# Four stacked graph layers on one core: partial sums of the projections copied by ScalarE from PSUM bank to PSUM bank, and layer 0's bias put into PSUM ahead of its products

## The chip, the cores and the metric

The kernel runs on one core of one Trainium2 chip. A core has five engines with queues of their own: TensorE (PE, with its weight loads shown as PEld), VectorE (DVE), ScalarE (ACT), GpSimd (POOL) and SyncE (SP, which here only issues DMAs). Matmul results land in PSUM, eight banks of 128 partitions by 512 fp32 elements; everything else lies in SBUF. The metric is the device time of one execution in microseconds, lower is better.

## What is computed

128 graphs of 128 nodes with 512 features pass four layers; after each layer the result is added to its input and every row is normalised:

```python
x = _layernorm(x + _L0_gnn_ref(x, adj, L0_kernel, L0_bias))   # relu(An @ x @ W0 + b0)
x = _layernorm(x + _L1_gnn_ref(x, adj, L1_W_qk, L1_W_v))      # softmax over nodes of a score, times x @ Wv
x = _layernorm(x + _L2_gnn_ref(x, adj, L2_W))                 # relu([x, Ar @ x] @ W2)
x = _layernorm(x + _L3_gnn_ref(x, adj, L3_W, L3_b))           # An @ (x @ W3 + b3)
```

All of it is fp32. The large cost is the product of a 128-node block of features with a 512 by 512 weight, once per graph in layers 0, 1 and 3 and twice in layer 2.

## The kernel before

Work comes in 32 tiles of four graphs. For each tile the kernel aggregates (`aggregate`: features times the normalised adjacency, PSUM tile `p_agg`, evicted by ACT into `agg`), or turns the features (`turn_x` through DMAs and DVE transposes, `turn_on_tensor` on TensorE, tiles `xT`), and then projects. The aggregations and turnings of layer L deliver the left operand of the projection of layer L.

The projections save one matmul in eight. Four graphs are taken as a 2 by 2 arrangement (two graph rows r, two pairs q), features and weights are split in halves, and instead of eight block products seven are made, named `B11, T1, B21, B22, T2, T3, T4`. Three of the left operands are sums of blocks, made by `left_sums`: S1 (for T1), S2 (for T2), S4 (for B22), each a chain step after the one before. POOL makes them in the ordinary tiles, DVE in some of the first and last ones. The sums of the weights are made once, by `weight_sums`. What the savings cost is that several results share partial sums: B11 goes into all four result blocks.

`project` (lines 583 to 650) does this for layers 0, 2 and 3 (`o0`, `o2`, `o3`; PSUM tiles `p_o`, 128x512, both pairs in one bank). Each product is 8 matmul records of 128x256 per weight (16 in layer 2, which has two weights). Before the change, the shared partial sum is carried through SBUF: ACT copies B11's sum into `s`, DVE then adds PSUM sums and SBUF sums:

```python
product(g, B11, True);  sa, sb = first(g, block)      # ACT copy (l0: two POOL adds of the bias)
product(q, T1, True);   u5 = q + sb                   # VectorE
product(v, T2, True);   u2 = v + sb                   # VectorE
product(q, B22, False); u2 = q + u2                   # VectorE
product(v, T3, False);  u5 = v + u5                   # VectorE
product(p, T4, ...);    sa = p + sa                   # VectorE, deferred to the tail
```

B21 is accumulated onto B11 in `g`, right after B11 where `early` holds (layers 0 and 2, and the last tile of layer 3), and after T1 elsewhere. The product T4 and what follows it is deferred: it is put on the list `tails` and run by `finish_tails()` after the next stage's B11. `fin` adds a result block to `x` (with relu in layers 0 and 2), `norm_stats` and `norm_last` normalise.

`l1_out` (lines 789 to 833) is the same scheme for the attention layer, with 320 output columns (256 values and 64 for the score), one bank for each pair q. It runs each of the seven products for both pairs before the next product (2 matmuls, 4 records of 128x320, per pair and product).

The order on TensorE is the order of the Python program. On the other engines it is not: `Plan` records all operations, and its list scheduler (`schedule`, `run`) orders DVE, ACT, POOL and SP by due times that it computes from estimated durations. Hooks (`{T1: [...]}`) place pieces of other stages between the products of a projection. In the ordinary tiles, layer 0 of tile t, layers 2 and 3 of tile t-1 and layer 1 of tile t are interleaved; `begin()` (tiles 0 to 2) and the lines after the loop (tile 31, `last`) have orders of their own. There, `l2_both` makes the aggregations and the turned features on TensorE and `left_sums` runs on DVE.

PSUM: the pool `ps_b` has five banks (`pb`), `ps_t` three (`pt`). At the start, `WARM` transposes of the identity run on TensorE while the first data are loaded.

Of the kernel before, what the change touches and what calls it, by code (L numbers as in the profile page):

```python
# [15 lines left out]
P = 128  # L16
# [9 lines left out]
DEG_EPS = 1e-6  # L26
WARM = 30

# [318 lines left out]
def estimate(engine, method, args, kw):  # L347

    out = args[0]
    n = out.idx.size if isinstance(out, Ref) else 0  # L350
    if engine == "tensor":
        return (max(109, 0.85 * n) if method == "transpose" else 2 * max(104, 0.833 * n + (2.5 if n > P else 5))), 100, 0, False
    if method == "dma_start":
        size = max(int(np.prod(v.shape)) if isinstance(v, bass.AP) else v.idx.size * 32 * len(v.quads) for v in args)
        return 470, Plan.LAND + size / 60, size, False
    if engine == "scalar":
        return (380 if method == "activation" else 160) + 0.83 * n, 0, 0, False
    if engine == "gpsimd":
        return (400 + 150 * n if ALU.pow in args else 250 + 2 * n), 0, 0, True
    if method in ("bn_stats", "tensor_reduce"):  # L360
        n = args[1].idx.size
    both = [v for v in args[1:] if isinstance(v, Ref) and v.idx.size == n and v.tile.args[3]["tag"] not in ("pb", "pt")]
    return 160 + (1.12 if len(both) > 1 else 1.04) * n, 0, 0, len(both) > 1
# [3 lines left out]
def kernel(  # L367
# [71 lines left out]
    make_identity(tc.nc, ident.real())  # L439
    p = ps_t.tile([P, C, P], FP, tag="pt", name="p_warm")  # L440
    for _ in range(WARM):
        nc.tensor.transpose(p[:, 0], ident, ident)
    nhalf = const.tile([P, G], FP, tag="nhalf", name="nhalf")
# [3 lines left out]
    w0_sb = weight(w0, "w0_sb", nc.sync)  # L447
    b0_sb = broadcast_row(b0, "b0_sb", nc.sync)
    wqk_sb = tp.tile([P, C, 2 * ATT], FP, tag="row", name="wqk_sb", bufs=1)
    for b in range(Q):  # L450
# [131 lines left out]

    def project(name, t, parts, first, c11, fin, hooks=None, after=lambda: None, pairs=(0, 1), early=True):

        hooks = hooks or {}
        qs = slice(pairs[0], pairs[-1] + 1)

        def region():  # L590
            return ps_b.tile([P, 2, H], FP, tag="pb", name=f"p_{name}_{t}")[:, qs]

# [5 lines left out]

        def product(p, k, fresh):
            with nc.unit():  # L600
# [9 lines left out]
        def block(tag):  # L610
            return tp.tile([P, 2, H], FP, tag=tag, name=f"{tag}_{name}_{t}", bufs=2 if tag == "s" else 1)[:, qs]

        g, q, v = region(), None, None
        product(g, B11, True)
        sa, sb = first(g, block)
        finish_tails()
        if early:
            product(g, B21, False)
            c11(g, block)
        q = region()  # L620
        product(q, T1, True)
        u5 = block("u5")
        nc.vector.tensor_tensor(u5, q, sb, ALU.add)
        if not early:
            product(g, B21, False)
            c11(g, block)
        v = region()
        product(v, T2, True)
        u2 = block("u2")
        nc.vector.tensor_tensor(u2, v, sb, ALU.add)  # L630
        product(q, B22, False)
        nc.vector.tensor_tensor(u2, q, u2, ALU.add)
        fin(0, 1, u2)
        norm_stats(name, t, 0, pairs)
        product(v, T3, False)
        nc.vector.tensor_tensor(u5, v, u5, ALU.add)
        fin(1, 1, u5)

        def tail():
            p = v  # L640
            if (name, t, pairs[-1]) == ("o3", last, 1):
                nc.vector.tensor_tensor(sa, v, sa, ALU.add)
                p = region()
            product(p, T4, p is not v)
            nc.vector.tensor_tensor(sa, p, sa, ALU.add)
            fin(1, 0, sa)
            norm_stats(name, t, 1, pairs)
            after()
# [3 lines left out]
    def half(z, r, h, pairs=(0, 1)):  # L652

        return z.rearrange("p (q r) f -> p q r f", r=2)[:, pairs[0]:pairs[-1] + 1, r, h * H:(h + 1) * H]

    def copy_first(p, block):
        s = block("s")
        nc.scalar.copy(s, p)
        return s, s


# [66 lines left out]
    def l0_out(t, hooks=None, pairs=(0, 1)):  # L728
        fin = relu_add(t, pairs)

        def bias(h):
            return b0_sb[:, None, h * H:(h + 1) * H].to_broadcast([P, len(pairs), H])

        def first(p, block):
            sa, sb = copy_first(p, block)[0], block("sb")
            nc.gpsimd.tensor_tensor(sb, sa, bias(1), ALU.add)
            nc.gpsimd.tensor_tensor(sa, sa, bias(0), ALU.add)
            return sa, sb

        def c11(p, block):  # L740
            c = block("u2")
            nc.vector.tensor_tensor(c, p, bias(0), ALU.add)
            fin(0, 0, c)

        project("o0", t, [("agg0", w0_sb)], first, c11, fin, hooks, pairs=pairs)

# [42 lines left out]
    def l1_out(t, hooks):  # L789
# [11 lines left out]
        st["v", t] = out  # L801
        s = out[1, 0]

        def region():
            return [ps_b.tile([P, 2, H], FP, tag="pb", name=f"p_v_{t}_{q}").rearrange("p a b -> p (a b)")[:, 0:V]
                    for q in range(2)]

        def product(p, k, fresh, then):
            for q in range(2):
                with nc.unit():  # L810
                    for c in range(2):
                        nc.tensor.matmul(p[q], a[k][:, q, c, :], wv_sb[:, c, k, :], start=(fresh and c == 0),
                                         stop=(c == 1), skip_group_check=True)
                then(p[q], q)
            for f in hooks.get(k, ()):
                f()

        def add(to, other):
            return lambda p, q: nc.vector.tensor_tensor(to[:, q, 0:V], p, other[:, q, 0:V], ALU.add)

        for r in range(2):
            nc.scalar.copy(out[r, 1][:, :, V], st["d", t].rearrange("p (q r) -> p q r", r=2)[:, :, r])
        g = region()
        product(g, B11, True, lambda p, q: nc.scalar.copy(s[:, q, 0:V], p))
        finish_tails()
        q5 = region()
        product(q5, T1, True, add(out[1, 1], s))
        product(g, B21, False, lambda p, q: nc.scalar.copy(out[0, 0][:, q, 0:V], p))
        v = region()
        product(v, T2, True, add(out[0, 1], s))  # L830
        product(q5, B22, False, add(out[0, 1], out[0, 1]))
        product(v, T3, False, add(out[1, 1], out[1, 1]))
        product(v, T4, False, add(s, s))

# [41 lines left out]
    def l2_out(t, hooks=None, pairs=(0, 1)):  # L876
        fin = relu_add(t, pairs)
        project("o2", t, [("xT2", w2x_sb), ("agg2", w2a_sb)],
                copy_first, lambda p, b: fin(0, 0, p), fin, hooks, pairs=pairs)


    def l3_agg(t):
        left("agg3", t)
        for g in (0, 1, 3, 2):
            aggregate("agg3", t, g, st["anT", t], 2 if g == 2 else 1)
        left_sums("agg3", t)

# [12 lines left out]
    def l3_out(t, hooks=None, left="agg3", pairs=(0, 1)):  # L900
        def fin(r, h, blk):
            z = half(st["x", t], r, h, pairs)
            nc.vector.tensor_tensor(z, blk, z, ALU.add)

        project("o3", t, [(left, w3_sb)], copy_first, lambda p, b: fin(0, 0, p), fin, hooks,
                after=lambda: store(t), pairs=pairs, early=t == last)

# [8 lines left out]
    def begin():  # L916
# [14 lines left out]
        l1_turn(0, turn_on_tensor, (1,))  # L931
        l1_out(0, {T3: [lambda: l1_turn(1, turn_on_tensor)]})
        l1_out(1, {B11: [lambda: l1_scores(0)], T1: [lambda: l1_softmax(0)], B21: [lambda: l1_add(0)]})
        l2_both(0, 0)
        l2_out(0, {B11: [lambda: l2_both(0, 1), lambda: prep(2)], T1: [lambda: l1_scores(1)], T2: [lambda: l1_softmax(1)], T3: [lambda: l1_add(1)]})
        l0_agg(2)
        l2_turn(1)
        l0_out(2, {B21: [lambda: l2_agg(1, 0)], T1: [lambda: l2_agg(1, 1)]})
        l3_agg(0)
# [10 lines left out]
    for t in range(2, NT):  # L950
        u = t - 1
        if t > 2:
            l0_out(t, {T1: [lambda: l2_agg(u, 0)], T2: [lambda: l2_agg(u, 1)]})
        tails.append(lambda: l1_turn(t))
# [7 lines left out]
        l3_bias(u)  # L962
        l3_out(u, {B11: [lambda: l1_softmax(t)], B21: [lambda: l1_add(t)]})
        if t < last:
# [4 lines left out]
    for q in range(2):  # L969
        l2_out(last, {B11: [lambda: l2_both(last, 1)], B21: [held]} if q == 0 else {B22: [lambda: l3_agg_pair(last, 0, nc.gpsimd)]}, (q,))  # L970
    for q in range(2):
# [37 lines left out]
```

## Time and profile before

| | before |
|---|---|
| time, median of 3 runs | 2437.45 us (2437.34 to 2437.57) |
| profiled execution, first to last instruction | 2436.3 us |
| PE busy | 2426.0 us (100%), 12462 records |
| PEld busy | 2090.2 us (86%) |
| DVE busy | 1637.9 us (67%) |
| POOL busy | 1219.3 us (50%) |
| ACT busy | 1004.2 us (41%) |
| mean granted TensorE clock | 1.000 |

The profile tells of one execution. Its span runs from the first to the last instruction and is 1.15 us shorter than the median time, which also holds what lies around the instructions. In the groups of the profile a line reads: engine, operation, output tile <- input tiles, shapes, count, busy time, mean duration of one in ns, idle time before it and who ended that idle time. All recorded operations carry the line of one helper (L323), so tiles tell them apart. Every fp32 matmul stands as two records; transposes stand as one.

### The profile page before, as it was taken

What the parts mean: (1) busy time and instruction counts of PE and PEld (TensorE: products, weight loads), DVE (VectorE), ACT (ScalarE), POOL (GpSimd) and SP (SyncE); (2) the same over time, 40 slices, a digit from 0 to 9 for tenths busy, and PEclk for the clock granted to TensorE, in tenths of its full rate; (3) what the DMA queues carried; (4) which work ended last, traced back from release to release, by engine and by line L of the source; (5) the groups of instructions that cost most, each with busy time, mean ns of one, the idle gap of its engine ahead of it and who ended that gap; (6) DMA issues with size and microseconds to landing.
All of it is one profiled execution on the core that took longest, in us unless ns stands there. A gap on an engine that the chain in (4) does not pass through costs nothing.

```text
span 2436.3 us, 35723 instructions
## 1 busy us (share of the span) xinstructions
PE 2426.0 (100%) x12462; PEld 2090.2 (86%) x12462; DVE 1637.9 (67%) x3398; ACT 1004.2 (41%) x2117; POOL 1219.3 (50%) x1580
## 2 busy tenths in 40 slices
PE   9999999999999999999999999999999999999998
PEld 8888888888888888888888888888888888888887
DVE  6766666677666677666776667666677666676656
ACT  4344333443434444344443444433443434444345
POOL 5364545545445554545455554545545455554543
PEclk9999999999999999999999999999999999999999
DMA  5234233442334433344333343333442334423220
GB/s 182 47 101 109 70 105 94 126 124 64 99 92 126 126 78 83 97 120 126 90 80 100 109 126 104 74 104 95 126 121 66 100 91 126 126 74 88 75 82 35
DMA packets 393267, 241.16 MB, mean 99 GB/s; under 512 B 140416, under 2 KB 358016, under 8 KB 393088
## 3 DMA queue, kind: packets, MB, share of 16 engines
q1 hardware_dynamic: 393088, 238.88, 36.4%
q8 instruction: 99, 1.62, 0.3%
q14 instruction: 80, 0.66, 0.1%
HBM read 126.62 MB, written 112.20 MB: 98 GB/s over the span
## 4 chain that ended last, share of the span: by engine, by line
PE 99%; ACT 1%; DVE 0%; POOL 0%; issue 0%; POOLq 0%; ACTq 0%; DVEq 0%
PE p_o L323 63%; PE p_v L323 20%; PE p_agg L323 14%; PE p_sc L323 1%; PE p_warm L323 0%; PE p_xT L323 0%; DVE x L323 0%; ACT x L323 0%; PE p_ws L323 0%; PE p_w L323 0%; ACT xT L323 0%; ACT xT1y L323 0%; POOL agg L323 0%; POOL last L323 0%; PE p_a L323 0%
## 5 line engine op out<-in xcount | busy, mean ns | idle before, releaser
L323 PE MATMUL p_o<-w_sb,agg 128*128 128x256 f32 x2048 | 471.0, 380 | 0.6 <-DVE u_o L323 0.6
L323 PEld LDWEIGHTS p_o<-w_sb,agg 128*128 128x128 f32 x2048 | 386.1, 190 | 52.0 <-POOL rstdv L323 1.0
L323 ACT COPY agg<-p_agg 128x512 f32<-128x512 f32 (+1 forms) x415 | 226.4, 554 | 371.9 <-PE p_agg L323 371.8
L323 PE MATMUL p_v<-wv_sb,xT 128*128 128x320 f32 x1024 | 291.6, 433 | 0.1
L323 DVE TENSOR_TENSOR v<-p_v,v 128x320 f32<-128x320 f32 x316 | 155.0, 491 | 174.7 <-PE p_v L323 174.4
L323 PE MATMUL p_o<-w2x_sb,xT 128*128 128x256 f32 x1024 | 263.1, 379 | 0.5 <-ACT xT L323 0.5
L323 PE MATMUL p_o<-w2a_sb,agg 128*128 128x256 f32 x1024 | 262.8, 379 | 0.0
L323 PEld LDWEIGHTS p_v<-wv_sb,xT 128*128 128x128 f32 x1024 | 192.0, 190 | 76.5 <-ACT xT L323 0.6
L323 PEld LDWEIGHTS p_agg<-anT,x 128*128 128x128 f32 x2048 | 238.7, 192 | 7.1 <-DVE anT L323 0.6
L323 PE MATMUL p_agg<-anT,x 128*128 128x128 f32 x2048 | 239.3, 275 | 0.3 <-DVE anT L323 0.3
L323 DVE TENSOR_TENSOR u_o<-p_o,u_o 128x512 f32<-128x512 f32 (+1 forms) x196 | 131.4, 672 | 149.1 <-PE p_o L323 149.1
L323 PEld LDWEIGHTS p_o<-w2x_sb,xT 128*128 128x128 f32 x1024 | 194.0, 190 | 30.7 <-ACT xT L323 1.0
L323 PEld LDWEIGHTS p_o<-w2a_sb,agg 128*128 128x128 f32 x1024 | 194.6, 190 | 26.4
L323 PE MATMUL p_v<-wv_sb,xT1s 128*128 128x320 f32 x768 | 217.2, 432 | 0.0
L323 PE MATMUL p_o<-w2x_sb,xT2s 128*128 128x256 f32 x768 | 197.1, 379 | 0.0
L323 PE MATMUL p_o<-w2a_sb,agg2s 128*128 128x256 f32 x768 | 197.1, 379 | 0.0
L323 ACT ACTIVATE x<-x,nmro,rstdo 128x512 f32<-128x512 f32 x256 | 195.2, 808 | 3.4
L323 PEld LDWEIGHTS p_v<-wv_sb,xT1s 128*128 128x128 f32 x768 | 145.7, 190 | 57.3
L323 PE MATMUL p_o<-w_sb,agg0s 128*128 128x256 f32 x768 | 180.8, 379 | 0.0
L323 DVE TENSOR_TENSOR u_o<-p_o,s_o 128x512 f32<-128x512 f32 (+1 forms) x132 | 88.5, 671 | 131.4 <-PE p_o L323 131.3
L323 PE MATMUL p_o<-w_sb,agg3s 128*128 128x256 f32 x744 | 170.8, 379 | 0.0
L323 DVE BATCH_NORM_STATS2 bno<-x 128x6 f32<-128x512 f32 x258 | 168.1, 683 | 3.3
(147 smaller groups left out, 4021.7 us busy)
## 6 DMA issues: line engine op xcount, KB each, us to landing
x<-in_x_dram SPq DMA_DIRECT2D x31, 1024.0 KB, 5.7
out_dram<-x SPq DMA_DIRECT2D x31, 1024.0 KB, 5.0
xT2s<-x SPq DMA_DIRECT2D x120, 256.0 KB, 2.5
xT2y<-xT2s SPq DMA_DIRECT2D x240, 128.0 KB, 3.3
xT1s<-x SPq DMA_DIRECT2D x120, 256.0 KB, 2.6
xT1y<-xT1s SPq DMA_DIRECT2D x240, 128.0 KB, 3.1
sa<-ana SPq DMA_DIRECT2D x120, 128.0 KB, 3.4
ya<-sa SPq DMA_DIRECT2D x120, 128.0 KB, 3.0
```

The lines of the kernel that those rows point to most:

```text
L323: op.ins = getattr(getattr(self.nc, op.engine), method)(*[v.real() if isinstance(v, Ref) else v for v in args], **{k: v.real() if isinstan ...
```

## The change

Partial sums are now carried inside PSUM. ACT copies a bank to another bank, and later products are accumulated onto the copy (matmuls without the start flag). In `project`, the product order becomes B11, (tails), T1, T2, B21, B22, T3, and T4 in the tail: `x` is a copy of B11's bank and takes T2, then `y`, a copy of `x`, takes B22, while `x` itself goes on to take T3 and T4; B21 goes onto B11's own bank. T1's result `f` is copied to SBUF by ACT and added by DVE once per result block of the last column. In layer 3 (`fold`) `f` is added to both blocks of `x` in one DVE operation instead, and the results are then added straight from PSUM. Layer 0's two bias halves (the second as a difference, made by one DVE subtraction at the start) are put into PSUM by two ACT copies ahead of B11 and T1; its two POOL additions per tile go away. The separate bank for the very last T4 goes away too.

`l1_out` takes each pair q as a generator of its own; the two are stepped in a fixed interleaving, fresh products use `ps_t`, copies use `ps_b`, and the last T4 becomes a tail, run by a new `finish_tails()` inside `l3_agg`. Hooks of the neighbouring stages are moved to other products. `WARM` goes from 30 to 28, and these transposes now write the banks of `ps_b`, in turn.

Over the program, ACT has 452 copies more (1195 for 743), DVE 551 tensor additions fewer (616 for 1167), POOL 64 fewer (1250 for 1314); TensorE has 6316 matmuls and transposes for 6318.

```diff
-WARM = 30
+WARM = 28
...
-    for _ in range(WARM):
-        nc.tensor.transpose(p[:, 0], ident, ident)
+    for i in range(WARM):
+        p = ps_b.tile([P, C, P], FP, tag="pb", name="p_warm") if i % C == 0 else p
+        nc.tensor.matmul(p[:, i % C], ident, ident, start=i % C == 0, stop=True, is_transpose=True, skip_group_check=True)
...
+    nc.vector.tensor_tensor(b0_sb[:, H:F], b0_sb[:, H:F], b0_sb[:, 0:H], ALU.subtract)
...
+        def copied(p):
+            to = region()
+            nc.scalar.copy(to, p)
+            return to
+
+        if seeds is None:
+            r = region()
+            product(r, B11, True)
+            x = copied(r)
+        else:
+            x, w = region(), region()
+            nc.scalar.copy(x, seeds[0])
+            nc.scalar.copy(w, seeds[1])
+            product(x, B11)
+            r = copied(x)
         finish_tails()
+        if seeds is None:
+            w = region()
+        product(w, T1, seeds is None)
+        f = block("f")
+        nc.scalar.copy(f, w)
+        if fold is not None:
+            fold(f)
+        product(x, T2)
+        y = copied(x)
+        product(r, B21)
+        fin(0, 0, r)
+
+        def last_column(p, r):
+            if fold is not None:
+                return fin(r, 1, p)
+            u = block("u")
+            nc.vector.tensor_tensor(u, p, f, ALU.add)
+            fin(r, 1, u)
+
+        product(y, B22)
+        last_column(y, 0)
         norm_stats(name, t, 0, pairs)
+        product(x, T3)
+        last_column(x, 1)
 
         def tail():
+            product(x, T4)
+            fin(1, 0, x)
             norm_stats(name, t, 1, pairs)
...
+        def one(q):                       # l1_out, one pair
+            p = fresh(B11, q)
+            x = copied(p, q)
+            yield
+            w = fresh(T1, q)
+            f = tp.tile([P, V], FP, tag="f", name=f"f_v_{t}_{q}", bufs=2)
+            nc.scalar.copy(f, w)
+            product(x, T2, q)
+            y = copied(x, q)
+            yield
+            product(p, B21, q)
+            end(0, 0, q, p)
+            yield
+            product(y, B22, q)
+            end(0, 1, q, y, f)
+            product(x, T3, q)
+            end(1, 1, q, x, f)
+            yield
+            product(x, T4, q)
+            end(1, 0, q, x)
+            yield
...
         for g in (0, 1, 3, 2):
             aggregate("agg3", t, g, st["anT", t], 2 if g == 2 else 1)
+            finish_tails()
...
-        l1_out(1, {B11: [lambda: l1_scores(0)], T1: [lambda: l1_softmax(0)], B21: [lambda: l1_add(0)]})
+        l1_out(1, {(T1, 0): [lambda: l1_scores(0)], (B21, 0): [lambda: l1_softmax(0)], (B22, 0): [lambda: l1_add(0)]})
...
-        l2_out(last, {B11: [lambda: l2_both(last, 1)], B21: [held]} if q == 0 else {B22: [lambda: l3_agg_pair(last, 0, nc.gpsimd)]}, (q,))
+        l2_out(last, {B11: [lambda: l2_both(last, 1)], T1: [held]} if q == 0 else {B22: [lambda: l3_agg_pair(last, 0, nc.gpsimd)]}, (q,))
```

## The prediction

> **What bounds the kernel now.** First the page: busy times and the chain that ended last.
>
> ```profile
> span 2436.3 us, 35723 instructions
> ...
> PE 2426.0 (100%) x12462; PEld 2090.2 (86%) x12462; DVE 1637.9 (67%) x3398; ACT 1004.2 (41%) x2117; POOL 1219.3 (50%) x1580
> ...
> PE 99%; ACT 1%; DVE 0%; POOL 0%; issue 0%; POOLq 0%; ACTq 0%; DVEq 0%
> ```
>
> TensorE is the chain. A busy PE may still hide gaps, so the second view is a window one period long in the middle (busy time and count of PE, PEld, DVE, ACT, POOL, then clock and DMA).
>
> ```profile
> 1200.00:1275.26 75.26, 75.26 (x388) 64.89 (x387) 50.66 (x106) 30.89 (x65) 38.23 (x50) 1.00 0.37 102
> ```
>
> The chain in order of time repeats every 75.26 us (p_v at 1227.39, then 1302.65), with PE busy throughout. That is its work: 224 records of p_o at 0.216 us apart (48.4), 56 of p_v at 0.269 (15.1), 96 of p_agg at 0.112 (10.7), scores and two small transposes 1.1. The third view, TensorE's waits, says what is left to gain:
>
> ```profile
> PE p_warm L323 <- POOL ident masks.py:199: 1.3, 1, 1.3
> PE p_xT L323 <- ACT xT1y L323: 0.7, 1, 0.7
> PE p_o L323 <- DVE u_o L323: 0.6, 1, 0.6
> PE p_o L323 <- ACT xT L323: 0.5, 2, 0.3
> PE p_agg L323 <- DVE anT L323: 0.3, 1, 0.3
> PE p_agg L323 <- ACT x L323: 0.2, 1, 0.2
> ```
>
> 3.6 us, all in the first tiles or the last; behind the last matmul there are 6.5 us more (2429.7 to 2436.3). The change keeps TensorE's work. It can win only there, and can lose wherever PE comes to wait.
>
> **Ordinary tiles: 0.** Per tile ACT gets 8 more copies of 128x512 and 6 of 128x320, DVE loses 12 additions of 128x512 and 6 of 128x320 and gets one of 1024 columns, POOL loses two bias additions. By the rows
>
> ```profile
> L323 ACT COPY s_o<-p_o 128x512 f32<-128x512 f32 (+1 forms) x98 | 56.5, 577 | 179.6 <-PE p_o L323 179.5
> L323 ACT COPY v<-p_v 128x320 f32<-128x320 f32 x128 | 54.5, 426 | 211.2 <-PE p_v L323 211.2
> L323 POOL TENSOR_TENSOR s_o<-s_o,b_sb 128x512 f32<-128x512 f32 x32 | 40.7, 1272 | 23.0 <-DVE x L323 23.0
> ```
>
> ACT goes from 30.9 to 30.9 + 8 x 0.58 + 6 x 0.43 = 38 of 75.26 us; DVE falls by 12 x 0.69 + 6 x 0.49 - 1.3 = 9.9, POOL by 2.5. None becomes the bound. No row shows a copy from PSUM to PSUM: the nearest are the 577 ns above and 611 ns from SBUF to SBUF (xT1y<-x); I take 0.58, bounds 0.43 (the short copy) and 0.81 (ACT's longest 128x512 operation).
>
> What counts is each hand-over: PE to ACT 0.25 us after the last matmul's slot (p_o's B11 ends at 1246.29, s_o starts at 1246.54), copy 0.58, back to PE 0.05 (anT ends at 8.87, p_agg starts at 8.92): 0.88. The copy of B11 must be done by T2, behind T1's 8 x 0.216 = 1.73, in layer 2 3.45; the copy y by B22, behind B21, the same. Slack 0.85 at the worst copy bound still 0.6, if ACT is free; the order of the changed program puts nothing long before these copies. In layer 1: 0.2 + 0.43 + 0.05 = 0.68 against 2.15 (two products of 1.08). The tightest wait is no copy: the second pair's T4 stands only 8 records of p_agg (0.89) behind T3, whose bank DVE must read first: 0.21 (T2's slot ends 1232.60, DVE starts 1232.81) + 0.49 + 0.05 = 0.75. Slack 0.14, DVE being idle there. Layer 2's T1 now comes without B21 (3.45 us) before it; its S1 on POOL ended 3.3 us early (xT2s 1274.88 + 1.27, T1 at 1279.49). DVE's lighter queue starts it earlier: about 1 us of slack stays.
>
> **Start: +0.2.** Two transposes fewer take 0.22 (two at the full rate, 0.11 as in p_a) to 0.43 (0.213, as most warm-ups ran) off the 12.60 at which B11 starts. But B11 now waits for a seed: b_sb, which landed at 3.97 + 8.3 = 12.25, is issued one place earlier (11.1, where the second w_sb landed), and its copy stands on ACT behind the third agg copy (11.90, now 11.7): 11.7 + 0.48 + 0.58 + 0.05 = 12.8. Bounds -0.2 and +0.5.
> [...]
>
> **Layer 1 of tile 0: +0.1.** T1 stands behind one pair's B11 (1.08), not two. S1 needs, after the last turn, 0.25 + 0.58 + 0.12 + 1.27 + 0.05 = 2.3, so PE waits 1.2, and 0.24 at T2 (S2 costs 1.32 against 1.08). In return the wait for xT1y (0.87 with its restart) and 0.4 of small ones go: ACT's chain there hung on POOL, which loses 1.27 of bias work.
>
> **Layer 1 of tile 1: +0.5, then +0.45.** Before, T1 at 64.34 stood 5.1 us after the last turn (59.19); now 2.15, at 61.3. xT1s ended at 62.17: 0.9 at most, 0.15 if POOL's weight sums before it move up. Tile 0's scores are hooked later: from p_w to layer 2's p_agg stood 11.0 us of PE work (66.55 to 77.54), now 9.8, and the chain (softmax, add, norm on ACT until 76.81) takes 10.3.
>
> **Layer 2 of tile 0: +0.6.** DVE's xT2s ends at 88.47; B21 covered it (86.86 to 90.32). Now only one T4 of layer 1 does: 86.86 + 1.08 = 87.94. Bounds 0.5 and 1.1.
>
> **Layer 3 of tile 0: +0.4.** S2 on POOL (131.16 to 132.79, T2 at 136.70) loses the cover of B21 (1.73) and of the tail moved ahead (1.73), and POOL also waits for DVE (0.72 in its row). Bounds 0 and 0.6.
>
> **Layer 2 of the last tile: +1.75.** The widest:
>
> ```profile
> 2389.55 1.03 PE L323 MATMUL p_o<-w2x_sb,xT 128*128 128x256 f32 x4
> ...
> 2390.83 0.69 DVE L323 TENSOR_TENSOR xT2s<-xT 128x512 f32<-128x512 f32 x1 [0.35 <-ACT xT L323]
> ...
> 2391.27 1.89 PE L323 MATMUL p_o<-w_sb,agg 128*128 128x256 f32 x8
> ...
> 2393.00 0.81 PE L323 MATMUL p_o<-w2x_sb,xT2s 128*128 128x256 f32 x3
> ```
>
> B21 (2389.55) and the held T4 (2391.27) cover S1, which ends at 2391.52. In the new order T1 comes first, and the held T4 behind it. PE would wait from 2389.55 to 2391.57; the s_o copy that stood before the last copies on ACT (0.26) comes after them now: 1.75, bounds 1.5 and 2.0.
>
> **End: +0.2.** The last T4 goes onto the bank that DVE is still reading: 0.2 + 0.42 + 0.05 = 0.7 of wait (before, a fresh bank). Behind it one DVE addition less: -0.45.
>
> **Dropped: -0.2.** The wait of 0.6 for u_o goes, but the next one, for ACT's x, is set by a chain that does not move.
>
> Sum: 0.2 + 0.1 + 0.5 + 0.45 + 0.6 + 0.4 + 1.75 + 0.2 - 0.2 = 4.0. On the profiled 2436.3 that is 2440.3; with the 1.15 us that the median lies above it, 2441.4. The lower bounds sum to +1.1, the upper to +6.5. The measurement tells 0.2% from no change, 4.9 us: 2432.6 to 2442.3.
>
> [...]
>
> **The rivals.** (1) Slower by a wait in every tile: T4 of layer 1 (slack 0.14) or S1 of layer 2 (about 1 us, behind a DMA whose landing varies). For it: the thin slack, and DVE's read being last. Against: PE had no such wait in 30 tiles at 0.33 of slack. It decides from 0.14 us of lateness on; 0.3 us late would be 30 x 0.3 = 9 on top, 2450. Chance 0.08. (2) Slower within the edges: the waits at first and last tiles come out at their upper bounds, 2443 to 2444; from +4.9 on it counts as slower. Chance 0.23. (3) Faster: the lighter DVE and POOL remove PE's early waits and the new ones stay hidden. All of PE's waits (3.6), the tail's 0.45, 0.4 of warm-up and the restarts (1.1) make -5.5 at most, 2432; the view of the last tile speaks against it. Chance 0.04. (4) The change does less than it says, because PE's order leaves the copies no use: nothing but the edges, which is the forecast.
>
> **How the numbers follow.** The forecast, within 0.2%, has 0.65; slower 0.08 + 0.23 = 0.31; faster 0.04. The range runs from the lower bounds (2438.5) to the upper (2444), and a little beyond toward rival 1: 2438.4 to 2444.6.
>
> **What would show it.** PE busy per 75.26 us unchanged and no wait of PE between 180 and 2300; ACT near 38, DVE near 41 us per period; a PE wait near 2391 for DVE's xT2s of 1.5 to 2 us, one of 0.7 before the last T4, some of 0.3 to 1.2 for POOL and DVE before 140. A PE wait repeated in each tile, or a copy beyond 1.4 us, would make it wrong.

## The result, and the profile after

The changed kernel takes 2443.21 us (median of 10 runs, 2442.83 to 2444.23) against 2437.47 us (10 runs, 2437.32 to 2438.33): ratio 1.0024, 95% interval 1.0014 to 1.0033. It is slower by 5.7 us, just past the 4.9 us that the prediction called measurable; the forecast was 2441.4 and the range 2438.4 to 2444.6. The profiled execution took 2442.89 us.

The page after: span, busy time, and the chain that ended last.

```profile
span 2441.1 us, 35406 instructions
...
PE 2426.6 (99%) x12460; PEld 2088.7 (86%) x12460; DVE 1365.1 (56%) x2847; ACT 1212.1 (50%) x2569; POOL 1156.4 (47%) x1516
...
PE 97%; POOL 1%; DVE 1%; ACT 1%; issue 0%; DMA 0%; POOLq 0%; ACTq 0%; DVEq 0%
```

TensorE's work is unchanged (2426.6 for 2426.0), ACT has 208 us more, DVE 273 us less, and the span is 4.8 us longer. The window of one period in the middle, columns as before:

```profile
1200.00:1275.26 75.26, 75.26 (x388) 64.89 (x387) 42.04 (x89) 37.47 (x79) 36.44 (x47) 1.00 0.40 102
```

PE is 100% busy, with the same 388 records in 75.26 us. 8.6 us less DVE and 6.6 us more ACT per tile are worth nothing. The 4.8 us stand in TensorE's waits:

```profile
PE p_o L323 <- DVE xT2s L323: 2.0, 2, 1.6
PE p_warm L323 <- POOL ident masks.py:199: 1.3, 1, 1.3
PE p_agg L323 <- ACT x L323: 1.0, 2, 0.7
PE p_v L323 <- POOL xT1s L323: 1.0, 1, 1.0
PE p_a L323 <- DVE ana L323: 0.7, 1, 0.7
PE p_o L323 <- POOL agg3s L323: 0.6, 1, 0.6
...
PE p_o L323 <- DVE x L323: 0.5, 1, 0.5
PE p_o L323 <- ACT p_o L323: 0.3, 1, 0.3
```

Each stands once or twice, so none belongs to an ordinary tile. Three of the eight name a sum of operands (xT2s, xT1s, agg3s), and one a bank that is still being read (x: the last T4). `p_agg` waits for x, normalised by ACT, once behind the later scores of tile 0 and once in the last tile. `p_warm` waits as before, and the 0.7 us ahead of `p_a` stand behind warm-ups that ended early in this execution; B11 began at 12.48 all the same, 12.60 before. Only `ACT p_o`, 0.3 us for the first seed, waits for a copy. The largest wait, on the timeline of the last tile:

```profile
2392.93 0.69 DVE L323 TENSOR_TENSOR xT2s<-xT 128x512 f32<-128x512 f32 x1 [0.35 <-ACT xT L323]
...
2393.66 0.69 DVE L323 TENSOR_TENSOR xT2s<-xT2s,xT 128x512 f32<-128x512 f32 x1
2393.68 0.30 PEld L323 LDWEIGHTS p_o<-w2x_sb,xT2s 128*128 128x128 f32 x2 [1.84 <-DVE xT2s L323]
```

T1 starts as S1 ends. DVE is no later than before relative to what it waits for (0.35 us of idle time in both); the products that had covered it, that is, had kept PE busy meanwhile, stand behind T1 now. The price of the new copies, from the groups by shape:

```profile
L323 ACT COPY p_o<-p_o 128x512 f32<-128x512 f32 x188 | 107.8, 573 | 249.3 <-PE p_o L323 249.3
L323 ACT COPY p_v<-p_v 128x320 f32<-128x320 f32 x128 | 52.5, 410 | 78.1 <-PE p_v L323 77.9
```

The copy from bank to bank takes 573 ns, where the prediction took 0.58 us, and the narrow one 410.

### The profile page after: what moved, and what is told of

It reads as the page before. It is cut to its first block, busy times and chain, and to the rows that moved or that the text cites. A ratio compares the mean times of both kernels' runs of the same rounds, so it can differ in the third digit from the quotient of the medians.

```text
span 2441.1 us, 35406 instructions
## 1 busy us (share of the span) xinstructions
PE 2426.6 (99%) x12460; PEld 2088.7 (86%) x12460; DVE 1365.1 (56%) x2847; ACT 1212.1 (50%) x2569; POOL 1156.4 (47%) x1516
## 3 DMA queue, kind: packets, MB, share of 16 engines
q1 hardware_dynamic: 393088, 238.88, 37.5%
## 4 chain that ended last, share of the span: by engine, by line
PE 97%; POOL 1%; DVE 1%; ACT 1%; issue 0%; DMA 0%; POOLq 0%; ACTq 0%; DVEq 0%
PE p_o L323 63%; PE p_v L323 19%; PE p_agg L323 14%; PE p_sc L323 1%; DVE x L323 0%; POOL xT1s L323 0%; POOL w_sb L323 0%; ACT xT L323 0%; ACT agg L323 0%; PE p_ws L323 0%; PE p_w L323 0%; ACT x L323 0%; DMA ana<-in_adj_dram 0%; POOL w2a_sb L323 0%; ACT xT2y L323 0%
## 5 line engine op out<-in xcount | busy, mean ns | idle before, releaser
L323 PE MATMUL p_o<-w_sb,agg 128*128 128x256 f32 x2048 | 476.8, 380 | 0.8 <-DVE x L323 0.5
L323 DVE SCALAR_TENSOR_TENSOR x<-p_o,x 128x512 f32<-128x512 f32 (+1 forms) x130 | 88.7, 683 | 405.2 <-PE p_o L323 402.4
L323 PE MATMUL p_v<-wv_sb,xT 128*128 128x320 f32 x1024 | 307.2, 433 | 0.0
L323 PEld LDWEIGHTS p_agg<-anT,x 128*128 128x128 f32 x2048 | 243.6, 192 | 11.8 <-DVE anT L323 0.4
L323 PE MATMUL p_agg<-anT,x 128*128 128x128 f32 x2048 | 244.2, 275 | 0.2 <-DVE anT L323 0.2
L323 ACT COPY p_o<-p_o 128x512 f32<-128x512 f32 (+1 forms) x196 | 110.7, 565 | 255.8 <-PE p_o L323 255.8
L323 PE MATMUL p_v<-wv_sb,xT1s 128*128 128x320 f32 x768 | 228.3, 433 | 1.1 <-POOL xT1s L323 1.0
L323 POOL TENSOR_TENSOR xT1s<-xT 128x512 f32<-128x512 f32 x32 | 40.7, 1273 | 277.4 <-DVE xT L323 250.4
```

The costliest lines, as they stand in the source:

```text
L323: op.ins = getattr(getattr(self.nc, op.engine), method)(*[v.real() if isinstance(v, Ref) else v for v in args], **{k: v.real() if isinstan ...
```

## The experiments

Each edits the changed kernel, except before_t1_first. Theory: the ordinary tiles cost nothing, and the loss is cover taken from operand sums, and one bank, at the first and last tiles (the edges). Rival: something per copy or per tile that the waits do not show.

**held_first.** One piece of PE work changes place.

```
-        l2_out(last, {B11: [lambda: l2_both(last, 1)], T1: [held]} if q == 0 else {B22: [lambda: l3_agg_pair(last, 0, nc.gpsimd)]}, (q,))
+        l2_out(last, {B11: [lambda: l2_both(last, 1), held]} if q == 0 else {B22: [lambda: l3_agg_pair(last, 0, nc.gpsimd)]}, (q,))
```

> The changed kernel, with one piece of TensorE work moved: in the last tile the held T4 of layer 3 (8 records of p_o, 1.73 us of PE) stands ahead of layer 2's T1 instead of behind it. Theory (the loss is cover taken from the operand sums): the wait of 1.76 us for DVE's xT2s at 2393.68 goes, with the 0.10 us of restart behind it; xT2s is then ready within 0.1 us of PE. Span 2441.1 - 1.8 = 2439.3, median near 2441.4. Rival (DVE's queue is late as a whole, so that the wait only moves to T2, which needs the next xT2s and agg2s): 0 to -0.5, median 2442.7 to 2443.2.

Measured: 2441.83 (2441.14 to 2442.48), ratio 1.0018 (1.0009 to 1.0026); span 2439.3, 1.8 less than the changed kernel's. T1 started at 2393.63 against S1's end, with a wait below 0.1. The span is the theory's number (the median is 0.4 above its 2441.4), and no wait reappeared at T2. One line of order was worth a quarter to a third of the loss (1.4 by the medians, 1.8 by the spans).

**t4_fresh.** The last T4 gets a bank of its own.

```
         def tail():
-            product(x, T4)
-            fin(1, 0, x)
+            p = x
+            if (name, t, pairs[-1]) == ("o3", last, 1):
+                fin(1, 0, x)
+                p = region()
+            product(p, T4, p is not x)
+            fin(1, 0, p)
```

> The changed kernel, but the very last T4 goes onto a PSUM bank of its own, and DVE adds both banks, one after the other, to the output rows. Theory: the wait before the last T4 (0.68 us, and 0.10 of restart) goes; DVE's additional 0.42 us runs beside T4's 0.86. Median 0.7 to 0.8 lower, 2442.4; TensorE's end 2434.9 - 0.78 = 2434.1, the tail stays at 6.2. Rival (the additional DVE operation lengthens the tail by as much): 0, median 2443.2.

Measured: 2443.25 (2442.84 to 2443.74), ratio 1.0024 (1.0014 to 1.0033): no gain. PE's wait is gone as expected (its last records follow one another at 0.216), yet the tail behind PE's end grew from 6.2 to 6.7 us. B11 of tile 0 also happened to start 0.76 later in this execution (below), so its times compare after taking 0.76 off. ACT's last sum of squares and POOL's instructions near the end, first of the changed kernel, then of this one:

```profile
2435.24 0.19 ACT L323 ACTIVATION_READ_ACCUMULATOR square<-x,last 128x1 f32 x1
...
2435.51 0.19 POOL L323 TENSOR_SCALAR last<-last 128x1 f32<-128x1 f32 x1 [1.56 <-ACT square L323]
...
2436.22 0.22 POOL L323 TENSOR_SCALAR rstdo<-mvo 128x1 f32<-128x1 f32 x1 [0.52 <-DVE mvo L323]
2436.40 0.57 POOL L323 TENSOR_TENSOR last<-last,nhalf 128x1 f32<-128x1 f32 x1
```

```profile
2436.03 0.19 ACT L323 ACTIVATION_READ_ACCUMULATOR square<-x,last 128x1 f32 x1
...
2436.35 0.22 POOL L323 TENSOR_SCALAR rstdo<-mvo 128x1 f32<-128x1 f32 x1 [1.61 <-DVE mvo L323]
2436.66 0.19 POOL L323 TENSOR_SCALAR last<-last 128x1 f32<-128x1 f32 x1
2436.93 0.57 POOL L323 TENSOR_TENSOR last<-last,nhalf 128x1 f32<-128x1 f32 x1
```

`last` belongs to the norm of the other row, which needs ACT's sum of squares and not T4; that sum did not move (2436.03 - 0.76 = 2435.27, for 2435.24). `rstdo`, T4's own norm, moved from 2436.22 to 2435.59 (2436.35 - 0.76). But POOL's queue now has the scaling of `last` behind `rstdo`, where the changed kernel had it ahead, and the power that follows for `last` moved only from 2436.40 to 2436.17. So in these two executions a wait of 0.78 was worth 0.23; the medians show nothing of it. The result is the rival's, by another way than it named.

**before_t1_first.** The kernel before with the new order alone in the last tile, and no copy between banks.

```
-                copy_first, lambda p, b: fin(0, 0, p), fin, hooks, pairs=pairs)
+                copy_first, lambda p, b: fin(0, 0, p), fin, hooks, pairs=pairs, early=(t, pairs) != (last, (0,)))
...
-        l2_out(last, {B11: [lambda: l2_both(last, 1)], B21: [held]} if q == 0 else {B22: [lambda: l3_agg_pair(last, 0, nc.gpsimd)]}, (q,))
+        l2_out(last, {B11: [lambda: l2_both(last, 1)], T1: [held]} if q == 0 else {B22: [lambda: l3_agg_pair(last, 0, nc.gpsimd)]}, (q,))
```

> The kernel before, with the products of layer 2's first pair in the last tile in the new order alone: B11, T1, held T4, B21, T2 instead of B11, B21, held T4, T1, T2. No copy between PSUM banks anywhere. Theory (the order makes the wait, not the copies): PE waits 1.6 to 1.8 us for DVE's xT2s near 2390, span 2436.3 + 1.8 = 2438.1, median 2439.2. Rival (the copies or the copied banks make the wait): no change, 2437.4 to 2437.5.

Measured: 2440.26 (2439.59 to 2441.93), ratio 1.0012 (1.0003 to 1.0021), +2.7. PE's wait before T1 is there (1.69 us at 2390.97), so the order makes it, not the copies; a second one (0.66 before a transpose, where the kernel before has 0.18) came with it. Seven of the 11 runs lie at 2439.6 to 2440.3, with spans of 2437.8 to 2438.5 where the theory had 2438.1; four lie at 2441.2 to 2441.9. The profiled one is of the latter, and its windows show why (first number behind the comma: PE busy; the last but two: granted clock):

```profile
2388.00:2391.00 3.00, 1.12 (x9) 0.89 (x9) 2.06 (x3) 2.74 (x7) 0.00 (x0) 0.97 0.00 0
2391.00:2394.40 3.40, 3.40 (x8) 2.76 (x9) 1.99 (x3) 2.57 (x8) 0.00 (x0) 0.52 0.02 5
```

Behind 3.00 us in which PE was busy for 1.12, the granted clock was 0.52 for the next 3.4 us, and eight records took 0.43 each: 1.6 us on top, as much as lies between the two groups of runs. That the other three runs of that group lost it at the same place is not shown; their mean granted clock (0.998, 0.998, 0.999) fits it. In the changed kernel, with the same wait but a busier stretch ahead of it (PE busy for all of 2388 to 2391, and for 1.80 of the 3.40 us behind), the clock stayed at 1.00. Ahead of the drop stand two waits of PE, 0.50 us before the transposes at 2388.36 and 1.52 before T1 at 2390.97, with eight transposes between them; what in them sets the clock is not shown.

**all_edges.** held_first and t4_fresh together, and the first tiles rearranged: in tile 0 both pairs' B11 ahead of layer 1's T1 and the operand sums of layers 1 and 3 on DVE; hooks of the new key "tails" run directly behind finish_tails().

```
         finish_tails()
+        for h in hooks.get("tails", ()):
+            h()
+        if t == 0:
+            next(a1)
...
-            left_sums("xT1", t)
+            left_sums("xT1", t, nc.vector if t == 0 else nc.gpsimd)
...
-        left_sums("agg3", t)
+        left_sums("agg3", t, nc.vector if t == 0 else nc.gpsimd)
...
-        l1_out(1, {(T1, 0): [lambda: l1_scores(0)], (B21, 0): [lambda: l1_softmax(0)], (B22, 0): [lambda: l1_add(0)]})
+        l1_out(1, {"tails": [lambda: l1_scores(0)], (T2, 0): [lambda: l1_softmax(0)], (B21, 0): [lambda: l1_add(0)]})
...
-        l2_out(0, {B11: [lambda: l2_both(0, 1), lambda: prep(2)], T2: [lambda: l1_scores(1)], B21: [lambda: l1_softmax(1)], T3: [lambda: l1_add(1)]})
+        l2_out(0, {B11: [lambda: l2_both(0, 1), lambda: prep(2)], "tails": [lambda: l1_scores(1)], B21: [lambda: l1_softmax(1)], T3: [lambda: l1_add(1)]})
```

> The changed kernel with the edges rearranged and the ordinary tiles left alone: the held T4 first; the last T4 on a fresh bank; in tile 0 both pairs' B11 of layer 1 ahead of T1, its operand sums on DVE (0.69 each for 1.27 on POOL); tile 0's operand sums of layer 3 on DVE; the scores of tiles 0 and 1 directly behind the finished tails, the softmax and the weighted addition of tile 0 one product earlier. Theory (in ordinary tiles the change costs nothing, all of the loss is at the edges): the excesses of PE's starts there go, 1.87 + 0.78 + 1.53 + 0.92 + 0.69 + 0.84 = 6.6 us, of which up to 1 may come back as smaller waits: median 2436.6 to 2437.6, no slower than before. Rival (the copies cost something in every tile that the waits do not show): at least 2440.

Measured: 2441.10 (2440.30 to 2441.78), ratio 1.0014 (1.0005 to 1.0023). The number is the rival's. All the waits aimed at went, but two came: 1.56 us at 67.78, where tile 0's weighted addition now stood too close behind its softmax, and 1.38 at 129.91. Of the first, 1.0 us is the last step of the softmax, the scaling of e_sb on DVE, which took 1.31 us and not 0.28 beside a 128x512 operation of POOL (66.30 to 67.56; copies_twice below has the same in nearly every tile). At the second, the earlier scores had changed the planner's order on SP: tile 1's transposes through DRAM stood behind four other transfers, and DVE, waiting 2.23 us for one, held up the addition that frees a bank. B11 of tile 0 started at 13.31. These losses are not something per tile, so neither side is decided; that led to the next three.

**seed_dve.** Tile 0's first seed on the other engine.

```
-            nc.scalar.copy(x, seeds[0])
+            if t == 0:
+                nc.vector.tensor_copy(x, seeds[0])
+            else:
+                nc.scalar.copy(x, seeds[0])
```

> The changed kernel, but in tile 0 DVE writes the first seed (the bias into x's bank) instead of ACT. In the profiles so far B11 started at 12.36, 12.48, 13.24 and 13.31 in four kernels that do not differ there: behind the seed, which stands on ACT behind copies that wait for a later adjacency block's landing (7.95 and 8.24 in the early two, 9.39 and 9.46 in the late two). Theory (the seed ties B11 to that landing, and this is why the time of the changed kernel scatters from 2442.8 to 2444.2): PE waits for no ACT before B11, which starts within 0.05 us of the last p_agg's slot; median 0.4 to 1.2 lower, 2442.0 to 2442.8, and the runs lie closer together. Rival (the landing holds PE itself up, the seed only stands beside it): 2443.2, as scattered.

Measured: 2443.32 (2442.72 to 2443.72), ratio 1.0023 (1.0014 to 1.0033): no gain, the runs still spread over 1.0 us (1.4 in the changed kernel), and PE waited 0.42 us for DVE instead of ACT. The tie is real, but DVE's queue has it too: its own operations on the second adjacency block stand ahead of the seed. ACT's queue, as t4_fresh shows it:

```profile
11.00 0.20 ACT L323 ACTIVATE dmn<-dm 128x4 f32<-128x4 f32 x1 [0.59 <-DVE dm L323]
11.12 0.57 ACT L323 COPY agg<-p_agg 128x512 f32<-128x512 f32 x1
...
12.60 0.59 ACT L323 COPY p_o<-b_sb 128x512 f32<-128x512 f32 x1
```

`dmn` comes from that block, and all behind it waits. With the block landing at 8.79, 9.26, 9.39 and 9.46, B11 started at 12.65, 13.12, 13.24 and 13.31: 3.85 later each time. In the executions where it landed before 8.5, B11 came 4.1 to 4.3 behind (12.36, 12.48, 12.68), so something else sets it there. In before_t1_first, which has no seeds, it landed at 9.43 and B11 started at 12.02. The seed on DVE gave 0.7 at a like landing (9.49, 12.63) and lost 0.6 again in small waits near 15, 30 and 41 us.

**copies_twice.** In both `copied` helpers, that of `project` and that of `l1_out`:

```
             nc.scalar.copy(to, p)
+            nc.scalar.copy(to, p)
```

> The changed kernel with each copy from PSUM bank to PSUM bank issued twice (the second writes the same values again): 14 more ACT copies per ordinary tile, 6 of 128x512 and 8 of 128x320, half of them... all without other use. Theory (a copy is hidden as long as hand-over and copy fit beside the product ahead of its reader: 0.88 and one more copy at 0.48 from start to start is 1.36 of 1.73): PE 75.26 us per period as before, ACT 37.5 + 6 x 0.48 + 4 x 0.33 = 41.7; median 2443.2, at most 0.5 more at the edges. Rival (each copy costs PE something, by the bank's port or by the order of ACT): the loss of 5.7 us comes a second time, 2449.

Measured: 2449.52 (2449.32 to 2449.98), ratio 1.0049 (1.0034 to 1.0064): 6.3 more, just what the rival said. (An ordinary tile has ten of these copies, six of 128x512 and four of 128x320, not the 14 that were expected.) But in the ordinary tiles PE waits for no copy. It starts 0.16 us late at one point in each ordinary tile, the transpose p_ws of the softmax's weights; the period is 75.45, and 30 x 0.19 = 5.7 of the 6.3 us are that. On the timeline:

```profile
1252.61 1.17 ACT L323 COPY p_o<-p_o 128x512 f32<-128x512 f32 x2 [1.48 <-PE p_o L323]
...
1253.69 0.35 ACT L323 ACTIVATE e_sb<-p_w,mn 4x128 f32<-4x128 f32 x1
...
1254.61 1.39 DVE L323 TENSOR_SCALAR e_sb<-e_sb,rsum 4x128 f32<-4x128 f32 x1
1254.65 1.27 POOL L323 TENSOR_TENSOR agg<-agg 128x512 f32<-128x512 f32 x1 [0.69 <-DVE rsum L323]
1256.11 0.14 PEld L323 LDWEIGHTS p_ws<-ident,e_sb 128*128 128x128 f32 x1 [0.38 <-issue]
```

The same place in the changed kernel, where p_w stands 3.32 us earlier:

```profile
1249.77 0.35 ACT L323 ACTIVATE e_sb<-p_w,mn 4x128 f32<-4x128 f32 x1
...
1250.44 0.28 DVE L323 TENSOR_SCALAR e_sb<-e_sb,rsum 4x128 f32<-4x128 f32 x1
...
1252.44 0.14 PEld L323 LDWEIGHTS p_ws<-ident,e_sb 128*128 128x128 f32 x1
```

The scaling of e_sb on DVE ends at 1250.72, 1.7 us ahead of p_ws. Here the second copy brings the exponential 0.6 us later and the scaling 0.85; there it meets POOL's 128x512 operation and ends 0.08 behind it, so 1.1 later again: 1.95 in all, more than the slack. Over all 32 tiles the scaling takes 1283 ns on average, 1.39 us in the 29 in which it is late, against 284 ns in the changed kernel. The traces of the two kernels fit this: the scaling takes 0.27 us where no POOL operation stands beside it (the changed kernel, 101.37), 0.28 with 0.19 of one to go (1250.44), 0.57 with 0.50 to go (1701.98) and 0.95 with 0.87 (the kernel before, 1247.69), and in the last two it ends 0.08 behind POOL's. Here DVE's row begins 0.04 us ahead of POOL's, and it is DVE that is late; at 194.12 in the kernel before, where it begins 0.07 ahead, it takes 0.27. What holds DVE up is not shown.

**twice_not3.** The same without layer 3, whose first copy stands ahead of the exponential.

```
             nc.scalar.copy(to, p)
+            if name != "o3":
+                nc.scalar.copy(to, p)
```

> As copies_twice, but in layer 3 each copy is issued once. There the doubled copy of B11 stood in ACT's queue ahead of the softmax's exponential; it came 0.48 us later, DVE's scaling of e_sb then met POOL's 128x512 operation and took 1.28 us instead of 0.28 in every tile, and PE waited 0.16 at p_ws in every tile. Theory (the loss of copies_twice is that one collision, the copies themselves are hidden): with 12 of 14 doubled copies left the ordinary tiles cost nothing again, period 75.26, e_sb back at 0.28; median 2443.2 to 2443.8. Rival (doubled copies cost PE wherever they stand): 12/14 of 6.3 us, 2448 to 2449.

Measured: 2443.62 (2442.79 to 2444.23), ratio 1.0025 (1.0015 to 1.0034). The period is 75.26 with ACT at 41.0, and e_sb takes 284 ns again. Eight of the ten copies per tile are doubled here, and the time is the changed kernel's within the noise (0.4 above it): the copies of the three other layers may be doubled for nothing, and the rival of a price per copy falls.

**t4_late.** In `one` of `l1_out`, the second pair's last addition before T4 twice:

```
             end(1, 1, q, x, f)
+            if q == 1:
+                end(1, 1, q, x, f)
```

> The changed kernel with one DVE addition too many per tile: the second pair's (1,1) block of layer 1 is added twice, so that DVE reads the bank of x for 0.44 us longer ahead of the T4 that is accumulated onto it. Theory (the slack of that T4 is 0.15 us: DVE ends at 1242.51, T4 starts at 1242.71, hand-over 0.05): 0.44 - 0.15 = 0.29 late, with 0.10 of restart 0.39 per tile, in 31 tiles 12 us: median 2455, a period of 75.65, and PE's largest wait is for DVE's v. Rival (DVE has room there, or the planner moves T4's neighbours so that PE does not notice): 2443 to 2444.

Measured: 2458.13 (2457.64 to 2458.43), ratio 1.0084 (1.0070 to 1.0098): 14.9 more, where 12 was expected. Two timelines of one place, the changed kernel's and this one's:

```profile
1242.02 0.49 DVE L323 TENSOR_TENSOR v<-p_v,f_v 128x320 f32<-128x320 f32 x1 [0.51 <-PE p_v L323]
...
1242.71 0.70 PE L323 MATMUL p_v<-wv_sb,xT 128*128 128x320 f32 x2
```

```profile
1248.99 1.02 DVE L323 TENSOR_TENSOR v<-p_v,f_v 128x320 f32<-128x320 f32 x2 [0.51 <-PE p_v L323]
...
1250.07 0.81 PE L323 MATMUL p_v<-wv_sb,xT 128*128 128x320 f32 x2 [0.22 <-DVE v L323]
```

DVE ends at 1242.51, T4 starts at 1242.71: 0.05 of hand-over (as from anT to p_agg, 8.87 to 8.92, in the kernel before) and 0.15 of slack. The second addition, onto the same output, takes 0.53 and not 0.44, so T4 is 0.38 late, with 0.10 of restart 0.48 in each of 31 tiles, 15 us. Rival 1 of the prediction (a wait in every tile) did not happen, but it stood 0.15 us away.

**copies_on_dve.** In both `copied` helpers:

```
-            nc.scalar.copy(to, p)
+            nc.vector.tensor_copy(to, p)
```

> The changed kernel with the copies from bank to bank issued on DVE instead of ACT: per ordinary tile 6 of 128x512 (0.69 by DVE's rows for p_o) and 4 of 128x320 (0.49), DVE 42.4 + 6.1 = 48.5 us of 75.26, ACT 37.5 - 5.1 = 32.4. Theory (what counts is not the share but that the copying engine is free at the moment, and DVE's queue holds runs of 1.3 to 2.8 us of row additions and statistics there): copies come later than the 1.73 us of cover allow in some places, PE waits of 0.3 to 2 us recur in every tile, 2455 to 2510. Rival (a copy of 0.25 + 0.69 + 0.05 = 0.99 us fits into 1.73 on any engine): 2443 to 2446.

Measured in two runs: 2515.81, ratio 1.0321 (1.0302 to 1.0340), 6 us above the theory's range and far from the rival's. The first of its waits of PE:

```profile
PE p_o L323 <- POOL xT2s L323: 39.2, 26, 2.9
PE p_o L323 <- DVE xT L323: 3.7, 7, 1.2
```

Again PE hardly waits for the copies themselves; it waits for POOL's sums, which wait for DVE. That the copies push DVE's transposes back, and the sums with them, is the reading of these waits, not tested by itself. DVE is busy 45.7 of 75.26 us there: no share of busy time tells this. A part of the loss is the clock: the granted clock was 0.50 for 6.8, 3.4 and 3.4 us behind three of the waits, of up to 2.9 us, late in the run (from 2317, 2399 and 2464 us on). An estimate from these durations is 7 of the 73 us.

**edges_again, edges_third.** all_edges less what it had lost: the scores of tile 1 and the weighted addition of tile 0 where the changed kernel has them; with the first seed on DVE (edges_again) or on ACT (edges_third).

Against all_edges:

```
-        l1_out(1, {"tails": [lambda: l1_scores(0)], (T2, 0): [lambda: l1_softmax(0)], (B21, 0): [lambda: l1_add(0)]})
+        l1_out(1, {"tails": [lambda: l1_scores(0)], (T2, 0): [lambda: l1_softmax(0)], (B22, 0): [lambda: l1_add(0)]})
...
-        l2_out(0, {B11: [lambda: l2_both(0, 1), lambda: prep(2)], "tails": [lambda: l1_scores(1)], B21: [lambda: l1_softmax(1)], T3: [lambda: l1_add(1)]})
+        l2_out(0, {B11: [lambda: l2_both(0, 1), lambda: prep(2)], T2: [lambda: l1_scores(1)], B21: [lambda: l1_softmax(1)], T3: [lambda: l1_add(1)]})
```

> The changed kernel with the edges rearranged once more, leaving out what all_edges lost again: the first seed by DVE; the held T4 ahead of T1; both pairs' B11 first and operand sums on DVE in layer 1 of tile 0; tile 0's scores directly behind the finished tails and its softmax one product earlier, but its weighted addition where the changed kernel has it; the scores of tile 1 where the changed kernel has them (moving them had moved transfers on SP's queue behind four others); operand sums of layer 3 of tile 0 on DVE; the last T4 on a fresh bank. Theory (the loss is all at the edges): from span 2441.1, 0.45 (seed) + 1.87 (T4 of layer 3) + 1.53 + 0.33 (layer 1 of tiles 0 and 1) + 0.84 (layer 3) + 0.23 (last T4) = 5.25 less, 2435.9, and with the 1.8 outside the span 2437.6 (2437.2 to 2438.4): level with the kernel before. Rival (something per tile): over 2439.5.

> As edges_again, but tile 0's seed by ACT again: with DVE B11 of tile 0 came 0.5 us earlier for the same landing, but PE then waited 0.3 to 0.5 us each near 30 and 41 us, where it does not in the changed kernel. Theory: 0.2 to 0.7 less than edges_again's 2438.6, so 2437.9 to 2438.4, still 0.4 to 0.9 above the kernel before: what is left are waits near 77 (0.6) and 88 us (0.7), which the kernel before doesn't have. Rival (the waits near 30 and 41 us have another cause): 2438.6 or more.

Measured: 2438.61 (2437.83 to 2439.86), ratio 1.0004 (0.9995 to 1.0013), and 2439.00 (2438.39 to 2439.44), ratio 1.0006 (0.9996 to 1.0015). The first is 0.2 above the theory's range and 0.9 below the rival's. Neither can be told from the kernel before (both intervals hold 1), with the copies in all 32 tiles. 4.2 to 4.6 of the 5.7 us were order and placing at the edges. In edges_third the waits near 30 and 41 us are gone as expected, but the median is 0.4 above edges_again's, not 0.2 to 0.7 below. Its span is equal (medians 2436.9 and 2436.8), and it has 2.1 us outside the span, as all_edges has, where other kernels have 1.8; the cause of that stays open. Left over are waits of 0.6 and 0.7 us near 76 and 87 us, together about what is still lost; no run takes them away. Neither version beats the kernel before.

## Why the prediction was right, and where it was off

What each stage added, as excess of PE's starts over their usual distances (0.216 for p_o, 0.269 for p_v, 0.112 for p_agg), after less before:

| step | predicted | measured |
|---|---|---|
| ordinary tiles | 0 | 0 |
| start | +0.2 | -0.1 |
| layer 1, tile 0 | +0.1 | +0.3 |
| layer 1, tile 1: T1, then scores | +0.5, +0.45 | +0.3, +0.6 |
| layer 2, tile 0 | +0.6 | +0.7 |
| layer 3, tile 0 | +0.4 | +0.8 |
| layer 2, last tile: T1 | +1.75 | +1.9 |
| other waits of the last tile | -0.2 | -0.4 |
| end | +0.2 | +0.6 |
| span (sum of the rows predicted; measured as a whole) | +4.0 | +4.8 |
| span to median | 1.15 | 1.8 |

The rows measured sum to 4.7; small excesses, the largest 0.16 at 129 us, make up the rest.

**Right.** Nothing in ordinary tiles; the places of the large waits, and the size of the largest to 0.15 us. Three came out 0.1 to 0.15 higher (the scores of layer 1, layer 2 of tile 0, T1 of the last tile), since behind each of these waits PE's second start came 0.10 late as well (0.32 us after the first for 0.216 at p_o, 0.213 for 0.112 at p_agg), which the sum left out except for what was dropped. ACT came to 37.5 us per period as forecast (38); DVE fell by 8.6 where the sum had 9.9, which mattered to nothing.

**The chances.** They were less right than the range: 0.65 stood on a change within 0.2%, and 0.31 on slower. The result, 0.24%, is in the second part by the prediction's own line at +4.9.

**Start.** The -0.1 is luck. It compares two single executions, of which the one before began B11 late (12.60, where before_t1_first has 12.02) and the one after early (12.48; in the nine executions with the seed on ACT B11 began at 12.36 to 13.31). The medians lie 0.9 us farther apart than these two executions do. How much of that is the start, and so more than the +0.2 of the step, no run measures.

**Layer 3 of tile 0.** The term was mis-sized: 0.8 for 0.4, and above its upper bound of 0.6. POOL waited 1.32 us for DVE's x ahead of S2, where 0.72 was taken from the kernel before, in which it stands ahead of S4.

**End.** The step said that one addition less on DVE takes 0.45 off the tail. The tail fell by 0.33 only, and PE lost 0.29 ahead of the last pair's T1, waiting for POOL's agg31s, which the step did not have; the kernel before lost 0.13 at the first pair's sum (agg30s) and nothing at the last one's. In t4_fresh most of the last T4's 0.78 was worth nothing, since the other row's norm stood close behind.

**From the span to the median.** This is the largest single miss. The 1.15 us between the shown profile and the median was taken as what lies around the instructions. In each run of the two kernels that gives both it is 1.7 to 1.9 us; the spans of 32 runs of the kernel before lie at 2435.4 to 2436.4, median 2435.8, and the shown profile (2436.3) is one of the longest: its warm-ups ran at 0.213 until 7.3 us, and p_a began at 7.54 where before_t1_first began it at 6.91. The changed kernel's own profile (2441.1) is one of its shortest (median 2441.45). So of the 1.8 us by which the forecast fell short some 0.65 is the base, 0.8 the sum of the waits, and 0.35 the distance of the changed kernel's shown profile, with its early B11 (12.48), from its median.

**The rivals.** Rival 2's time (2443 to 2444) was met, though not by its way: the waits came to +4.8 where its upper bounds gave +6.5, and the base did the rest. Rival 1 did not happen; 0.15 us of slack kept it away (t4_late). Nothing speaks for rival 3. Rival 4's part, that the copies have no use where PE sets the order, holds: DVE lost 8.6 us per tile, and no wait in an ordinary tile went away, for there was none.

## What to carry to other kernels

Here one engine was busy throughout, and 8.6 us per tile less work on another changed nothing but the edges. Look there for which operand was covered by which product, because the new order, free in the ordinary tiles, uncovered the first and the last ones (1.9 us before one product). Check the cover of every chain that the engine taking over the work also serves, not only of the moved work: one more copy was free in three layers and cost 0.2 us per tile in the fourth, by way of an exponential and of two engines that met. And read a baseline from more than one execution before adding an offset to its span.

## What the runs showed of the hardware

- ACT copied 128x512 from bank to bank in 573 ns (p_o<-p_o), from a bank to SBUF in 578 (f_o<-p_o), and from SBUF to a bank in 603 (p_o<-b_sb), all in the changed kernel: 30 ns apart.
- A 4x128 operation on DVE took 1.39 us where it met a 128x512 operation of POOL (29 of 32 tiles of copies_twice), 0.95 beside one with 0.87 us to go (the kernel before, 1247.69), and 0.27 with none beside it (the changed kernel, 101.37).
- The granted clock was 0.50 for 3.4 us behind 3.4 us in which PE had been busy 1.51 (before_t1_first), and for 3.4 to 6.8 us behind 1.25, 1.29 and 1.45 of 3.4 us (copies_on_dve). Behind 1.80 of 3.4 us it stayed at 1.00 (the changed kernel). No single wait was longer than 2.9 us.
- On transposes alone their distance fell from 0.213 to 0.109 us at some time between 4.2 and 7.3 us in 13 executions; p_a of tile 0 began between 6.8 and 7.5 us with it.
- After most waits PE's second start came 0.10 us late as well (0.32 us after the first for 0.216 at p_o, 0.373 for 0.269 at p_v, 0.213 for 0.112 at p_agg); 0.05 to 0.08 at some transposes and products (0.168 for 0.109 at p_xT, 43.65, and 0.291 for 0.216 at p_o, 2379.49, both in the kernel before).
